# One hand-ordered instruction stream in another order: a cross-attention and MLP block on one core

## The chip, the cores and the metric

The kernel runs on 1 core of one Trainium2 chip. The metric is the device time of one execution in microseconds (us), lower is better. The core has a matrix engine (TensorE, PE in the profile), a vector engine (VectorE, DVE), a scalar engine (ScalarE, ACT), a general engine (GpSimd, POOL) and a queue engine for transfers (SyncE, SP). Each engine runs its own instructions in the order in which the program wrote them, and waits on semaphores for what the others have to deliver.

## The reference

One transformer block in fp32 for 4 batches of 512 rows of width 512, with 16 heads of 32 and a hidden width of 2048:

```python
x = layer_norm(hidden_states, ln1_w, ln1_b)
q, k, v = x @ q_w + q_b, enc @ k_w + k_b, enc @ v_w + v_b      # split into 16 heads of 32
scores = where(mask, q @ k.T / sqrt(32), finfo.min)
out = softmax(scores) @ v                                      # heads side by side again
hidden = (out @ cproj_w + cproj_b) + hidden_states
y = gelu(layer_norm(hidden, ln2_w, ln2_b) @ fc_w + fc_b, approximate=True)
return hidden + y @ proj_w + proj_b
```

## The kernel before

The work is cut into 16 windows w: window w is head group w % 4 (4 heads, 128 columns) of batch w // 4. After four windows a batch goes through the output projection, the second layernorm, the first MLP product (8 chunks c of 256 hidden columns) and, at the end of the kernel, the second MLP product. Batches overlap: while the windows of one batch are in attention, the MLP of the batch before fills TensorE.

The order of everything is a string. `ORDER` (line 60 on) is a list of tokens; the loop at the end of `xattn_block` starts, for each new token, the generator that the table `takes` gives for its name, and each time that the token stands in the string, the generator runs to its next `yield`. So one token is one step, and the place of its n-th occurrence is where its n-th step is written. The schedule is manual: each engine's instructions come in the order of the string, and the waits follow from what a step reads and overwrites. Buffers come from first-in first-out rings (`Ring`): 8 PSUM banks `accs` (a `take` at the first step, a `done` at the last reader), 6 row buffers `rows_of`, 3 staging buffers `stage`. With another order a step can therefore get another bank, and wait for another step to free it.

The tokens that the change and the prediction speak of (step n of a token is written x:4:1.3, counted from 0):

- `k:w`, `q:w`, `v:w` (`prep_k`, `prep_q`, `prep_v`): the projections of a window, 8 matmuls (v: 32) on TensorE, then one ScalarE instruction that frees the bank. `wk:w`, `wq:w`, `wv:w` are the loads of their weights, issued by SP (L331).
- `u:w:t` (`scores`, L516): 8 matmuls for 128 rows t of window w, into four banks. `x:w:t` (`exps`): four steps, each a VectorE instruction (L524) that reads a bank, adds the mask and frees the bank, and a ScalarE exponential (L529).
- `r:w:t` (`turn`): VectorE stream transposes of the exponentials (L537, L544), for odd t also of the reciprocal sums (L541, L547). `d:w:h` (`stay`): POOL copies of a half h of the result (L554). `e:w:h` (`exchange`): 12 SP transfers for the half, swap to swap, that carry the other parts between partitions. `a:w` (`attend`): 32 matmuls (L572) on the exchanged tiles, then one VectorE product (L580). The exchanged tile has one buffer, so the exchange of window w+1 waits for the product of window w.
- `c:b:t` (`cproj`): output projection of 128 rows, with a VectorE add and a POOL transfer to memory. `s1:b`/`s2:b`, `r1:b`/`r2:b`, `n1:b`/`n2:b`, `t1:b:d`/`t2:b:d`: statistics (VectorE, L345), reciprocal roots (POOL, L353 to L361), normalisation (VectorE, L366) and transposes (PE L373, then a VectorE L381 or ScalarE evacuation) of the first and second layernorm. For batches 1 to 3 the first layernorm is applied on an already transposed input: `lb:b` loads the statistics broadcast over partitions (SP, tile `xn<-sd`), `na:b` applies them on POOL (L414), `wa:b` scales on ScalarE (L425).
- `lf:b:c` loads fc weights, `fs:b:c` adds up blocks of them (POOL; VectorE for chunks 2 to 7 of the last batch), `y:b` adds up blocks of the activations (VectorE), `f:b:c` (`fc`, L627) is the product in the Strassen-Winograd form with 7 products for 8 (5 steps of 4 or 8 matmuls), `j:b:c` (`joins`, L652 on) puts its results together on ScalarE and VectorE in a staging buffer, `g:b:c` (`gelu`) applies Gelu there and stores it to memory (a POOL transfer, L674, `gd<-st`), which frees the staging buffer when it has landed.
- `ps`, `pt`, `gs`, `xs`: VectorE sums for the second MLP product `P:b:n` (two levels of the same form), `pj` and `J` its joins.

Of the kernel before, what the change touches and what calls it, by code (L numbers as in the profile page):

```python
# [20 lines left out]
P = 128  # L21
# [51 lines left out]
u:1:3 x:1:3 x:1:3 r:1:2 lt:1 x:1:3 x:1:3 r:1:3 r:1:3
u:2:0 x:2:0 k:4 r:1:3 r:1:3 d:1:0 v:2 d:1:0 d:1:1 k:4 v:4 v:4 v:4 x:2:0 x:2:0 x:2:0 d:1:1 e:1:0 e:1:0 e:1:0
u:2:1
u:2:2 x:2:1 x:2:1 r:2:0 e:1:1 x:2:1 r:2:1 e:1:1 e:1:1 fs:0:1 x:2:1 k:5 r:2:0 r:2:1 x:2:2 wq:5 v:1 fs:0:1 x:2:2 x:2:2
  lb:1 lb:1 r:2:1 r:2:1 k:5 r:2:2 wk:6 na:1 v:5 v:5 x:2:2 lt:1 wv:7 a:1 a:1
u:2:3
u:3:0 x:2:3 r:2:2 wv:6 na:1 e:2:0 na:1 e:2:0 x:2:3 x:2:3 x:2:3 r:2:3 r:2:3 r:2:3 k:6 r:2:3 e:2:0 e:2:1 e:2:1 x:3:0
  e:2:1 na:1 wa:1 d:2:0 wa:1 lf:0:3 wa:1 v:7 d:2:0 wa:1 x:3:0 x:3:0  # L80
u:3:1 q:4 x:3:0 q:4 x:3:1 x:3:1 r:3:0 x:3:1 r:3:0 x:3:1 r:3:1 r:3:1 r:3:1 r:3:1 q:5 wq:7 wv:9 q:5 k:6
u:3:2 x:3:2 x:3:2 d:2:1 x:3:2 x:3:2 d:2:1 a:2 a:2 d:3:0
u:3:3 v:7 wk:7
u:4:0 r:3:2 lx:2 x:3:3 q:7 d:3:0 x:3:3 x:3:3 x:3:3 r:3:2 r:3:3 r:3:3 r:3:3 r:3:3 m:1 k:7 x:4:0 q:7 x:4:0 x:4:0 x:4:0
# [840 lines left out]
```

## Time and profile before

| | |
|---|---|
| median of 3 runs | 757.0 us (755.46 to 757.13) |
| profiled execution, its own time | 760.23 us |
| span of the profiled execution | 758.4 us |
| mean granted TensorE clock | 0.997 |
| PE busy | 747.4 us, 99% of the span, 4413 matmuls |
| DVE busy | 604.9 us, 80% |
| ACT busy | 395.5 us, 52% |
| POOL busy | 374.0 us, 49% |
| transfers | 162.12 MB, mean 214 GB/s |

The profile is of one execution. It lists each engine's busy time, the waits with the instruction that ended them (`<-` names the releaser, which is inferred from semaphore events), the instructions in order of time, and the granted TensorE clock as a share of full speed. A matmul counts as busy while it is in the engine's pipeline, so a busy PE is not a PE at its peak: where the operands of consecutive matmuls come late, the group is only longer. Rows of a timeline hold the start in us from the span's start, the duration, engine, source line, operation, tiles (out<-in), the count of instructions that follow each other, and in brackets the idle time of the engine before them.

### The profile page before, as it was taken

Reading aid. Unit: us, or ns where it says so; the run is one execution under the profiler, and the core shown is the slowest. Engines: PE = TensorE matmul, PEld = TensorE weight load, DVE = VectorE, ACT = ScalarE, POOL = GpSimd, SP = SyncE. Lnnn points to the kernel's source line nnn. Section 1 sums busy time; section 2 is a strip of 40 time slices with the busy share of each in tenths; the row PEclk is TensorE's granted clock in tenths of the full one; section 3 lists DMA queues with packets and bytes.
Section 4 is the critical chain, followed back from the end, with each engine's and each line's share of the span. In section 5 each row is a group of like instructions: output and inputs, shape, how many; then the busy total and the mean of one; then the engine's idle time right before and its main releaser. Section 6 shows DMA issues by size and latency. Waiting matters only on the chain.

```text
span 758.4 us, 13011 instructions
## 1 busy us (share of the span) xinstructions
PE 747.4 (99%) x4413; PEld 526.9 (69%) x4413; DVE 604.9 (80%) x1193; ACT 395.5 (52%) x943; POOL 374.0 (49%) x401
## 2 busy tenths in 40 slices
PE   9999999999999999999999999989999999999998
PEld 6564634457665457674655677674889999999997
DVE  3899989998887979877789876745867998787782
ACT  2666675466887756869566868830334311111110
POOL 1176763744794676497637838581411013231241
PEclk9999999999999999999999999999999999999999
DMA  8689889966979788687796979996455467898485
GB/s 295 230 236 263 236 206 245 237 178 186 271 191 249 193 268 213 175 237 226 189 253 216 253 247 247 261 261 221 147 154 165 159 232 144 233 206 240 96 177 117
DMA packets 72129, 162.12 MB, mean 214 GB/s; under 512 B 11960, under 2 KB 24656, under 8 KB 70400
## 3 DMA queue, kind: packets, MB, share of 16 engines
q1 hardware_dynamic: 56864, 131.44, 60.7%
q0 software_dynamic: 15056, 29.84, 15.7%
q8 instruction: 35, 0.57, 0.3%
q14 instruction: 30, 0.25, 0.1%
q10 hardware_dynamic: 144, 0.02, 0.0%
HBM read 73.95 MB, written 25.18 MB: 131 GB/s over the span
## 4 chain that ended last, share of the span: by engine, by line
PE 67%; DVE 3%; issue 3%; DMA 2%; POOL 1%; ACT 1%; DVEq 0%; ACTq 0%; POOLq 0%
PE acc L627 43%; PE acc L516 5%; PE acc L572 5%; PE acc L447 4%; PE acc L491 4%; PE acc L502 3%; PE acc L479 3%; DMA gd<-st 2%; DVE ptt L524 1%; DVE swap L537 0%; POOL wsum L337 0%; DVE ptt L337 0%; DVE st L334 0%; DVE xn L334 0%; PE acc L373 0%
## 5 line engine op out<-in xcount | busy, mean ns | idle before, releaser
L529 ACT ACTIVATE ptt<-ptt,mn 128x512 f32<-128x512 f32 x256 | 182.7, 715 | 85.8 <-DVE mn L524 85.1
L524 DVE CUSTOM_DVE_ANT_0 ptt<-acc,mix 128x512 f32<-128x512 f32 x256 | 164.8, 680 | 24.9 <-PE acc L516 17.5
L554 POOL COPY swap<-swap 32x1088 f32<-32x1088 f32 x128 | 141.5, 1105 | 72.3 <-DVE mix L580 41.4
L537 DVE STREAM_TRANSPOSE swap<-ptt 128x1024 f32<-128x1024 f32 x64 | 79.0, 1235 | 5.8 <-ACT ptt L529 1.6
L544 DVE STREAM_TRANSPOSE swap<-ptt 128x1024 f32<-128x1024 f32 x64 | 77.9, 1220 | 0.6 <-ACT ptt L529 0.6
L652 ACT COPY xn<-acc 128x128 f32<-128x128 f32 x75 | 18.8, 268 | 107.0 <-PE acc L627 101.2
L516 PE MATMUL acc<-pbt 32*128 32x512 f32 x512 | 73.5, 626 | 1.1 <-ACT pbt L494 0.8
L627 PE MATMUL acc<-ys,wsum 128*128 128x256 f32 x256 | 65.8, 390 | 2.6 <-ACT st L652 2.6
L674 POOL DMA_DIRECT2D gd<-st x32 | 24.1, 761 | 85.5 <-ACT st L672 61.4
L502 PEld LDWEIGHTS acc<-ptt,ext 128*128 128x128 f32 x512 | 59.0, 192 | 8.6 <-DVE mn L524 3.5
L652 ACT COPY st<-acc 128x256 f32<-128x256 f32 x96 | 34.4, 367 | 52.1 <-PE acc L627 45.5
L334 DVE TENSOR_TENSOR st<-acc,st 128x512 f32<-128x512 f32 (+1 forms) x64 | 34.6, 547 | 33.8 <-ACT st L652 23.1
L502 PE MATMUL acc<-ptt,ext 128*128 128x128 f32 x512 | 60.3, 276 | 0.0
L572 PE MATMUL acc<-swap,mix 128*32 128x512 f32 x512 | 58.2, 595 | 1.0 <-POOL swap L554 0.6
L627 PEld LDWEIGHTS acc<-ys,wsum 128*128 128x128 f32 x256 | 48.3, 193 | 15.4 <-ACT st L652 6.6
L479 PE MATMUL acc<-ext,ptt 128*128 128x512 f32 x128 | 58.9, 603 | 0.0
L627 PE MATMUL acc<-yT,pbt 128*128 128x256 f32 x240 | 57.4, 384 | 0.6 <-DVE yT L381 0.6
L491 PE MATMUL acc<-ext,ptt 128*128 128x512 f32 x128 | 57.8, 597 | 0.0
L447 PE MATMUL acc<-mix 128*128 128x512 f32 x128 | 57.3, 598 | 0.0
L672 ACT ACTIVATE st<-st,vec 128x512 f32<-128x512 f32 x64 | 43.9, 718 | 22.1 <-DVE st L334 21.6
L627 PEld LDWEIGHTS acc<-yT,pbt 128*128 128x128 f32 x240 | 44.3, 190 | 15.1 <-DVE mn L524 4.7
L811 POOL DMA_DIRECT2D swap<-xn x18 | 21.9, 1431 | 62.7 <-DVE xn L334 17.7
(129 smaller groups left out, 1386.2 us busy)
## 6 DMA issues: line engine op xcount, KB each, us to landing
swap<-swap SPq DMA_DIRECT2D x384, 136.0 KB, 2.4
gd<-st POOLq DMA_DIRECT2D x32, 512.0 KB, 4.6
swap<-gd SPq DMA_DIRECT2D x12, 1024.0 KB, 6.6
pbt<-fc_w_dram SPq DMA_DIRECT2D x40, 256.0 KB, 4.2
xn<-x_dram SPq DMA_DIRECT2D x32, 256.0 KB, 4.7
ext<-fc_w_dram SPq DMA_DIRECT2D x24, 256.0 KB, 3.1
swap<-xn POOLq DMA_DIRECT2D x18, 256.0 KB, 4.8
ptt<-k_w_dram SPq DMA_DIRECT2D x16, 256.0 KB, 5.1
```

The source lines that it names most:

```text
L447: nc.tensor.matmul(acc, oT[:, g, ts(t, P)], wc[:, g, :], start=(g == 0), stop=(g == NG - 1))
L479: nc.tensor.matmul(acc, S["wk", w][:, d, :], eT[:, d, :], start=(d == 0), stop=(d == ND - 1))
L491: nc.tensor.matmul(acc, S["wq", w][:, d, :], xT[:, d, :], start=(d == 0), stop=(d == ND - 1))
L502: nc.tensor.matmul(acc[:, ts(t, P)], eT[:, d, ts(t, P)], S["wv", w][:, d, :], start=(d == 0), stop=(d == ND - 1),)
L516: nc.tensor.matmul(sc, S["qT", w][r, ts(qt, P)], S["kT", w][r, :], start=True, stop=True)
L524: nc.vector.tensor_tensor_reduce(out=s, in0=accs.held["s", w, qt, h], in1=mb, scale=1.0, scalar=FMAX, op0=ALU.add, op1=ALU.min, accum_out=mn,)
L529: nc.scalar.activation(s, s, AF.Exp, bias=mn, scale=-1.0, accum_out=S["sums", w][:, qt, h : h + 1])
L537: nc.vector.transpose(*two_heads[0])
L544: nc.vector.transpose(*two_heads[1])
L554: nc.gpsimd.tensor_copy(pT[ts(i, HD), i], tb[ts(i, HD), i])
L572: nc.tensor.matmul(av[ts(h, HD), :].rearrange("p (i a q) -> p i a q", i=2 * NI, a=2), v[:, t, ts(h, HD)], p[:, t, h], start=(t == 0), stop ...
L627: nc.tensor.matmul(o, x[:, k], y[:, k], start=(k == 0 and not more), stop=(k == n - 1), skip_group_check=more)
```

## The change

Only the string `ORDER` differs. Both strings hold the same 2367 tokens, each as often, so that every engine runs the same instructions on the same kinds of tile; what differs is the order on each engine, and through the rings which of the equal buffers a step gets. On TensorE 343 of its 458 blocks of matmuls stand at the same place of the sequence. The parts that the prediction speaks of (a `u` token at the head of a line is only how the string is broken into lines):

```diff
--- before.py
+++ after.py
@@ -58,171 +58,167 @@
 ORDER = """
...
-u:2:2 x:2:1 x:2:1 r:2:0 e:1:1 x:2:1 r:2:1 e:1:1 e:1:1 fs:0:1 x:2:1 k:5 r:2:0 r:2:1 x:2:2 wq:5 v:1 fs:0:1 x:2:2 x:2:2
-  lb:1 lb:1 r:2:1 r:2:1 k:5 r:2:2 wk:6 na:1 v:5 v:5 x:2:2 lt:1 wv:7 a:1 a:1
...
-u:3:0 x:2:3 r:2:2 wv:6 na:1 e:2:0 na:1 e:2:0 x:2:3 x:2:3 x:2:3 r:2:3 r:2:3 r:2:3 k:6 r:2:3 e:2:0 e:2:1 e:2:1 x:3:0
-  e:2:1 na:1 wa:1 d:2:0 wa:1 lf:0:3 wa:1 v:7 d:2:0 wa:1 x:3:0 x:3:0
-u:3:1 q:4 x:3:0 q:4 x:3:1 x:3:1 r:3:0 x:3:1 r:3:0 x:3:1 r:3:1 r:3:1 r:3:1 r:3:1 q:5 wq:7 wv:9 q:5 k:6
-u:3:2 x:3:2 x:3:2 d:2:1 x:3:2 x:3:2 d:2:1 a:2 a:2 d:3:0
-u:3:3 v:7 wk:7
-u:4:0 r:3:2 lx:2 x:3:3 q:7 d:3:0 x:3:3 x:3:3 x:3:3 r:3:2 r:3:3 r:3:3 r:3:3 r:3:3 m:1 k:7 x:4:0 q:7 x:4:0 x:4:0 x:4:0
-  e:3:0 s1:2 fs:0:0
-u:4:1 x:4:1 x:4:1 d:3:1 k:7 e:3:0 e:3:0 r:4:0 e:3:1 e:3:1 e:3:1 x:4:1 x:4:1 r:4:0
-u:4:2 x:4:2 x:4:2 fs:0:0 v:6 le:2 lf:0:2 lf:0:2 r:4:1 r:4:1 x:4:2 x:4:2 r:4:1 r:4:1 le:2 d:3:1 r:4:2
-u:4:3 a:3 a:3 x:4:3 x:4:3 r:4:2 c:0:0 c:0:0 d:4:0 x:4:3 lh:0 d:4:0 wq:6 x:4:3 fs:0:0 r:4:3 r:4:3 r:4:3 r:4:3 c:0:1
-  c:0:0 lx:2
-u:5:0 x:5:0 v:5 s2:0 x:5:0 x:5:0 x:5:0 c:0:1 c:0:2 s1:2 d:4:1 le:2 c:0:2 wk:8 wq:9 e:4:0 e:4:0 e:4:0 s2:0 s2:0 cb:0
...
-u:5:1 x:5:1 x:5:1 c:0:3 v:6 v:6 c:0:1 k:8 e:4:1 r:5:0 r:5:0 e:4:1 e:4:1 c:0:2 fs:0:0 c:0:3 q:6 s2:0 x:5:1 x:5:1 c:0:3
...
+u:2:2 d:1:1 v:4 e:1:0 r:2:0 r:2:0 x:2:1 e:1:1 e:1:1 e:1:1 lb:1 x:2:1 r:2:1 r:2:1 v:5 v:5 k:5 x:2:2 r:2:1 r:2:1 x:2:2
+  lb:1 wk:6 a:1 x:2:2 x:2:2 wq:5 r:2:2 wv:7 na:1 na:1 na:1 a:1 d:2:0 lt:1
...
+u:3:0 e:2:0 wa:1 e:2:0 k:6 v:7 wa:1 r:2:3 wa:1 r:2:3 e:2:0 r:2:2 r:2:3 e:2:1 e:2:1 e:2:1 x:3:0 x:3:0 na:1 x:3:0 lf:0:3
+u:3:1 x:3:1 lx:2 wa:1 q:4 q:4 x:3:0 x:3:1 s1:2 d:2:0 r:3:0 x:3:1 x:3:1 q:5 wk:8 r:3:0 wq:7 r:3:1 r:3:1 wv:9 d:2:1
+  d:2:1 r:3:1 k:6
+u:3:2 r:3:1 x:3:2 q:5 a:2 x:3:2 x:3:2 x:3:2 a:2 v:7 r:3:2
+u:3:3 x:3:3 q:7 d:3:0 x:3:3 x:3:3 x:3:3 r:3:2 r:3:3 r:3:3 r:3:3 r:3:3
+u:4:0 m:1 x:4:0 q:7 x:4:0 wk:7 x:4:0 x:4:0 k:7 d:3:0
+u:4:1 x:4:1 x:4:1 d:3:1 e:3:0 e:3:0 e:3:0 r:4:0 r:4:0 k:7 e:3:1 e:3:1 d:3:1 e:3:1 lf:0:2 x:4:1
+u:4:2 x:4:2 x:4:2 x:4:1 r:4:1 x:4:2 r:4:1 r:4:1 r:4:2 fs:0:0 v:6 x:4:2 le:2 le:2
+u:4:3 fs:0:0 fs:0:0 r:4:1 a:3 a:3 x:4:3 x:4:3 le:2 x:4:3 x:4:3 c:0:1 d:4:0 d:4:0 r:4:3 wq:9 r:4:3 r:4:3 r:4:3 wv:8
+  c:0:0 c:0:1 r:4:2 d:4:1 c:0:0 s2:0
+u:5:0 x:5:0 x:5:0 x:5:0 le:2 s1:2 c:0:2
+u:5:1 d:4:1 lh:0 x:5:1 x:5:1 c:0:3 e:4:0 e:4:0 s2:0 e:4:0 wq:6 v:6 x:5:0 q:6 fs:0:0 e:4:1 r:5:0 e:4:1 lx:2 lx:2 r:5:1
...
-u:7:1 x:7:1 x:7:1 j:0:2 lb:2 na:2 wk:10 k:10 lf:0:4 lf:0:4 na:2 k:10 v:10 e:6:0 e:6:0 wa:2 e:6:0 f:0:2 lt:2 lt:2 j:0:2
-  s1:3 f:0:4 r:6:3 d:6:0 j:0:4 fs:0:2 lf:0:6 fs:0:4 r:7:0 x:7:1 x:7:1 r:7:0
...
+u:7:1 lf:0:4 v:10 e:6:0 e:6:0 e:6:0 x:7:1 k:10 k:10 fs:0:2 lf:0:6 wa:2 lt:2 lt:2 f:0:2 j:0:2 d:6:0 r:7:0 f:0:4 x:7:1
+  x:7:1 j:0:4 lh:1 d:6:1 x:7:1 j:0:2
...
-u:14:1 d:13:1 x:14:1 x:14:1 x:14:1 r:14:0 q:15 q:15
-u:14:2 x:14:2 g:1:5 lf:2:1 n2:2 f:1:7 t2:2:3 e:13:1 t2:2:2 lf:2:3 f:1:7 x:14:1 t2:2:0 x:14:2 fs:2:0 j:1:7 t2:2:0
-  e:13:1 t2:2:1 f:1:7 r:14:1 x:14:2 g:1:6 j:1:7 lp:1 x:14:2 t2:2:1 j:1:7 f:2:0 r:14:1 f:1:7 t2:2:3 t2:2:2 fs:2:0 f:2:1
...
-  fs:3:1 c:3:0 lp:5 P:0:2 P:0:2 j:2:7 s2:3 c:3:3 s2:3 g:2:7 lr ps:4 fs:3:1 c:3:2 s2:3 g:2:5 fs:3:0 s2:3 ps:4 c:3:2
-  c:3:3 g:2:5 fs:3:1 r2:3 n2:3 j:2:7 pj:0:1 g:2:7 xs:0:4 g:2:5 n2:3 g:2:6 n2:3 n2:3 t2:3:0 t2:3:0 t2:3:1 t2:3:2 t2:3:3
-  t2:3:3 t2:3:1 f:3:1 t2:3:2 f:3:0 y:3 g:2:7 y:3 y:3 fs:3:0 fs:3:0 f:3:1 ps:6 j:3:1 ps:0 f:3:1 hd:0 j:3:0 gs:0:6 j:3:1
...
-  f:3:2 j:3:0 j:3:0 f:3:3 gs:0:7 pt:6 f:3:0 lf:3:2 ps:6 pj:0:2 P:0:6 j:3:0 g:3:0 j:3:3 fs:3:3 fs:3:3 fs:3:3 fs:3:3
-  j:3:0 g:3:0 g:3:0 fs:3:2 fs:3:2 f:3:3 fs:3:2 g:3:1 ps:2 f:3:3 P:0:5 j:3:3 f:3:3 j:3:3 j:3:3 f:3:2 f:3:3 g:3:1 j:3:2
-  f:3:2 pt:4 j:3:2 fs:3:2 ps:4 pt:4 pt:5 pt:4 P:0:4 hd:0 J:0:1 f:3:2 pj:0:4 pt:4 j:3:3 j:3:3 j:3:2 lf:3:5 g:3:3 f:3:5
...
+u:14:1 x:14:1 x:14:1 r:14:0 x:14:1 x:14:1 q:15
+u:14:2 x:14:2 q:15 f:1:7 f:1:7 j:1:7 x:14:2 d:13:1 e:13:1 e:13:1 n2:2 g:1:6 t2:2:3 t2:2:0 e:13:1 r:14:1 lf:2:3 t2:2:2
+  t2:2:1 t2:2:0 g:1:5 fs:2:0 f:1:7 lf:2:4 x:14:2 j:1:7 x:14:2 t2:2:1 f:2:0 j:1:7 f:1:7 lf:2:3 lp:1 t2:2:3 fs:2:0
+  fs:2:0 f:2:1 j:1:7 g:1:7 fs:2:1 j:2:0 lf:2:2 t2:2:2 y:2 fs:2:1 lf:2:6 y:2 y:2 j:1:7 g:1:7 f:2:1 j:2:1 r:14:1 r:14:1
...
+  j:2:6 la:0:4 xs:0:4 cb:3 P:0:1 a:15 a:15 ps:0 j:2:6 g:2:6 c:3:1 c:3:0 c:3:1 lp:3 ps:2 fs:2:7 la:0:2 la:0:7 c:3:2
+  ps:2 j:2:7 lf:3:1 j:2:7 cb:3 cb:3 gs:0:5 gs:0:6 pt:6 c:3:3 f:2:7 c:3:0 j:2:5 j:2:5 s2:3 j:2:7 s2:3 lp:6 lf:3:0
+  lf:3:0 g:2:5 xs:0:4 fs:3:0 g:2:6 lp:5 P:0:2 lf:3:1 fs:3:1 fs:3:1 c:3:1 c:3:0 lr P:0:2 pj:0:1 g:2:7 g:2:5 ps:4 fs:3:1
+  c:3:2 s2:3 c:3:3 ps:4 s2:3 c:3:2 c:3:3 j:2:7 r2:3 n2:3 g:2:7 fs:3:1 n2:3 n2:3 n2:3 xs:0:4 g:2:7 fs:3:0 t2:3:0 t2:3:1
+  t2:3:1 g:2:5 t2:3:2 t2:3:3 t2:3:0 f:3:1 t2:3:3 t2:3:2 y:3 y:3 y:3 j:3:1 fs:3:0 f:3:0 f:3:1 f:3:1 ps:6 ps:6 fs:3:0
...
+  lf:3:3 j:3:1 j:3:0 j:3:0 g:3:1 f:3:3 f:3:0 j:3:1 fs:3:3 j:3:0 j:3:0 f:3:2 P:0:6 g:3:0 fs:3:3 fs:3:3 fs:3:3 g:3:0
+  ps:0 lf:3:2 fs:3:2 fs:3:2 fs:3:2 j:3:3 f:3:3 f:3:3 P:0:5 g:3:0 j:3:3 f:3:3 j:3:3 j:3:3 f:3:2 j:3:2 f:3:2 hd:0 f:3:3
+  ps:2 ps:6 P:0:4 fs:3:2 j:3:2 g:3:1 f:3:2 J:0:1 ps:4 pt:4 pt:4 j:3:3 pt:4 pt:4 pt:5 lf:3:5 lf:3:5 g:3:3 f:3:5 j:3:2
...
```

The new order moves, among others: `lb:1` directly behind the exchange `e:1:1`; `na:1`'s last step behind the first copies `d:2:0`; `wa:1` between the exponentials of window 3; `s1:2` from window 4 into `u:3:1`; `q:7` in front of `u:4:0`'s matmuls; `wq:6` behind `e:4:0`, and `q:6` in front of `k:8`; `r:7:0` in front of three exps of `x:7:1`; `x:14:1`'s last step in front of `n2:2`'s; the second `gs:0` sum in front of `s2:3`, `fs:3:1` behind `r2:3`; `f:3:2`'s third step in front of `f:3:3`'s last.

260 lines of the change are left out of this document (127 added, 133 removed).

## The prediction

> **What bounds the kernel now.** I read the page's busy times first, then the waits of TensorE, then the stretches in which its stream is not dense, and there the other engines.
>
> ```profile
> PE 747.4 (99%) x4413; PEld 526.9 (69%) x4413; DVE 604.9 (80%) x1193; ACT 395.5 (52%) x943; POOL 374.0 (49%) x401
> ```
>
> TensorE (PE) is busy for 747.4 of the span's 758.4 us. The change leaves its 4413 matmuls as they are, so no order can save more than the time in which the matmul stream is stretched or stands still. The largest standstill is in the list of waits:
>
> ```profile
> PE acc L627 <- ACT st L652: 2.6, 2, 2.3
> ```
>
> One wait of 2.3 us, and it cost more than itself:
>
> ```profile
> 500.57 4.48 PE L627 MATMUL acc<-ys,wsum 128*128 128x256 f32 x12 [2.27 <-ACT st L652]
> ```
> ```profile
> 100.00:128.00 28.00, 27.02 (x148) 11.97 (x150) 27.33 (x62) 19.09 (x51) 13.34 (x13) 1.00 0.84 212
> 497.20:500.60 3.40, 1.14 (x6) 0.68 (x5) 3.37 (x4) 0.45 (x2) 3.11 (x3) 1.00 0.83 260
> 501.60:505.00 3.40, 3.40 (x10) 2.65 (x9) 0.39 (x1) 0.74 (x2) 3.28 (x3) 0.51 0.97 219
> ```
>
> The first row is the fc product that waited (batch 2, chunk 6); the others are stretches of the span with the busy time of PE, PEld, DVE, ACT and POOL, then the granted clock. After the wait TensorE ran 3.40 us at 0.51 of its clock, which lost about half of them, some 1.6; with the 2.3 of standstill (and a little at its edges) the accident cost about 4.1. The profiled execution took 760.2 (span 758.4 and 1.8 around it), 3.2 above the median of 757.0, so I take it that the timed runs have not all had this accident. My sum is made on the profiled execution and applied to the median: the 4.1 are no part of the gain, because the changed order leaves the same ACT copy behind the same staging store there.
>
> The stretch from 100 to 128 shows the other kind of loss. TensorE counts as busy for 27.02 of 28 us, but VectorE (DVE) has 27.33 of 28, and matmuls of the scores are spread out while they wait for their banks:
>
> ```profile
> 101.45 1.14 PE L516 MATMUL acc<-pbt 32*128 32x512 f32 x8
> 103.22 3.64 PE L572 MATMUL acc<-swap,mix 128*32 128x512 f32 x32 [0.64 <-POOL swap L554]
> 106.80 3.62 PE L516 MATMUL acc<-pbt 32*128 32x512 f32 x16
> 110.35 3.70 PE L491 MATMUL acc<-ext,ptt 128*128 128x512 f32 x8
> 113.89 3.60 PE L479 MATMUL acc<-ext,ptt 128*128 128x512 f32 x8
> 117.41 2.37 PE L516 MATMUL acc<-pbt 32*128 32x512 f32 x14
> 120.12 1.12 PE L516 MATMUL acc<-pbt 32*128 32x512 f32 x2 [0.34 <-DVE mn L524]
> 121.17 3.84 PE L502 MATMUL acc<-ptt,ext 128*128 128x128 f32 x32
> 124.94 1.58 PE L516 MATMUL acc<-pbt 32*128 32x512 f32 x8
> 126.45 1.92 PE L572 MATMUL acc<-swap,mix 128*32 128x512 f32 x16
> ```
>
> Starts and lengths of groups of matmuls. Two score blocks (x16) hold TensorE from 106.80 to 110.35, two more (14 and 2) from 117.41 to 121.17, one from 124.94 to 126.45: 8.8 us for five. A block of 8 that waits for nothing takes 1.1 (the first row), so 3.3 are lost, with the 0.64 in front of attend of window 2 some 3.9. This is the largest place that an order can repair. Two smaller ones are at 433-443 and 540-546.
>
> **The change part by part.** Nothing is added or removed; each engine keeps its instructions and durations. So every term below is a step that comes earlier or later, against what waits for it.
>
> *(1) 78 to 128.* Four moves work together. Before, the two broadcast loads of the layernorm statistics (lb:1) stand behind a weight load; now they follow the last exchange of window 1.
>
> ```profile
> 78.67 0.58 SPq L331 DMA_DIRECT2D ptt<-q_w_dram  x1
> 79.36 0.86 SPq L331 DMA_DIRECT2D xn<-sd  x2
> ...
> 108.27 15.12 SPq L331 DMA_DIRECT2D swap<-swap  x24
> ```
> ```profile
> 83.77 1.27 POOL L414 TENSOR_TENSOR ext<-ext,xn 128x512 f32<-128x512 f32 x1 [5.22 <-DMA xn<-sd]
> ```
> ```profile
> 98.67 1.25 DVE L537 STREAM_TRANSPOSE swap<-ptt 128x1024 f32<-128x1024 f32 x1 [1.25 <-POOL swap L554]
> ```
>
> GpSimd (POOL) waited 5.22 us for that load, and from 83.77 to the last copy of window 2 (which attend at 103.22 waits for) it has no gap; the load issued 0.7 earlier (79.36 to 78.67) starts its chain 0.7 earlier. VectorE's 1.25 us wait at 98.67 is for the second of these copies, and POOL's order there (three multiplications, copies, the fourth multiplication, copies) keeps the same work in front of it: 98.0. In the wait VectorE now does layernorm statistics of batch 2 (s1:2.0, 0.84), which stood at 118.5. So VectorE is 0.7 ahead up to 118 and 1.55 from there. Attend of window 2 starts a little earlier, until the landing of its own exchange is the limit; VectorE reaches its result 0.7 earlier, and the exchange of window 3, which waits for that, starts at 107.6 and not at 108.27.
>
> ```profile
> swap<-swap SPq DMA_DIRECT2D x384, 136.0 KB, 2.4
> ```
>
> Its 24 issues take 15.1 us, the last lands 2.4 after its issue: 125.2 before, 124.5 after. On TensorE projection q:7 (3.5 us) moves in front of the first score block of window 4, so that the banks have come free when it is reached; the blocks of 117 to 126 follow VectorE, 0.7 to 1.55 earlier. Attend of window 3 starts at about 124.6, against 126.45: a gain of **1.9**. If the load does not land earlier, only the statistics' 0.84 and part of the bank time are left (0.4); if the landing is no limit, 2.6.
>
> *(2) 180 to 216.* VectorE's first transposes of window 7 now stand in front of three exps (x:7:1.1 to 1.3), not behind one of them.
>
> ```profile
> 206.15 1.25 DVE L537 STREAM_TRANSPOSE swap<-ptt 128x1024 f32<-128x1024 f32 x1 [0.99 <-DMA pbt<-fc_w_dram]
> ```
>
> They wait until 206.15 for an exchange to have read their buffer. One exp (0.6) that filled time before this wait now comes behind it, and the score block and fc product that take its bank are that much later: a loss of 0 (the exchange is early) to 0.6; with the wait of 0.99 that the row shows most of the exp would have fitted in it, so I take the middle, **0.3**.
>
> *(3) 432 to 446.*
>
> ```profile
> 433.59 0.69 DVE L524 CUSTOM_DVE_ANT_0 ptt<-acc,mix 128x512 f32<-128x512 f32 x1 [1.62 <-PE acc L516]
> 434.21 0.08 DVE L524 DVE_READ_ACCUMULATOR2_ANT mn<- 128x1 f32 x1
> 434.21 1.64 DVE L366 TENSOR_SCALAR xn<-xn,mv,rs 128x512 f32<-128x512 f32 x1
> ```
> ```profile
> 440.49 0.70 PE L627 MATMUL acc<-yT,pbt 128*128 128x256 f32 x2 [0.60 <-DVE yT L381]
> ```
>
> VectorE idles for 1.62 until score block u:14:2 has run, then normalises the last row (n2:2.3). An exp of the block before (x:14:1.3) moves into the idle time, and on TensorE one fc step (0.87) moves in front of the transposes that need the row. The row is 0.6 later, its need 0.9 later; behind it VectorE has one exp less, so the transposed blocks come 0.5 to 1.6 earlier. The 0.60 wait goes, with about 0.3 of stretch on either side of it: **1.1** gained (0.2 lost to 1.3 gained, by how long the normalisation takes).
>
> *(4) 522 to 546.*
>
> ```profile
> 536.79 0.55 DVE L366 TENSOR_SCALAR xn<-xn,mv,rs 128x512 f32<-128x512 f32 x1 [1.22 <-POOL rs L361]
> ...
> 538.18 2.31 DVE L366 TENSOR_SCALAR xn<-xn,mv,rs 128x512 f32<-128x512 f32 x3
> ```
> ```profile
> 540.55 1.64 PE L373 MATMUL acc<-ident,xn 128*128 128x128 f32 x13 [0.34 <-DVE xn L366]
> ```
>
> Two g-sums instead of one stand ahead of the statistics (1.1 more), but c:3:3 and a weight-side sum go behind, so the statistics end within a few tenths of the same time. A result join then fills part of the 1.22 wait, and a sum between the first and second normalisation goes behind the fourth: the four rows follow each other and end 0.9 sooner than 540.5, and TensorE's 0.34, with as much again in the next fc step, goes: **0.6** gained (1.4 lost to 1.0 gained).
>
> *(5) The Gelu store at 559 to 566.*
>
> ```profile
> DMA to landing us min/median/max: 3.3/4.6/8.9
> ```
>
> The row is that of the 32 staging stores. The join that needs a store landed is called earlier by TensorE, since f:3:2.2 now precedes the 8 matmuls of f:3:3.4; the store is issued earlier by about as much, since its chunk's last fc step and join move up too. The stall has the same condition as before: **0** (0.5 either way).
>
> *(6) Weight wq:6.* Its load stood ahead of the exchange of window 4; now it stands behind the first half of that exchange, and q:6 is called 3.4 us earlier, in front of k:8.
>
> ```profile
> 131.78 9.16 SPq L331 DMA_DIRECT2D swap<-swap  x12
> 140.98 0.58 SPq L331 DMA_DIRECT2D ext<-encT_dram  x1
> ```
> ```profile
> 149.83 3.60 PE L491 MATMUL acc<-ext,ptt 128*128 128x512 f32 x8
> ```
> ```profile
> DMA to landing us min/median/max: 2.8/4.7/8.8
> ```
>
> The last row is that of the 48 k, q and v weight loads. Half an exchange takes 9.2 us of SyncE's (SP's) queue. With the 1.6 to 1.9 of part (1), the load is issued at about 139.3; q:6 is due at 149.83 less the 3.5 of k:8 (as k:7, 113.89 to 117.41) less 1.9, 144.4. So it is hidden up to 5.1 us of landing, above the median of 4.7: cover, but 0.4 of it. I charge **0.5** for this and the other steps whose margin has shrunk under a microsecond (v:2, v:5, c:0:1, called 3.4 earlier); bounds 0 and the rival's price.
>
> Sum: 1.9 - 0.3 + 1.1 + 0.6 + 0 - 0.5 = 2.8 us. 757.0 - 2.8 = 754.2, or 757.4 on the profiled execution's own time with the accident at 498, 753.3 without.
>
> **What speaks against (3) and (4).**
>
> ```profile
> 434.06 0.73 POOL L674 DMA_DIRECT2D gd<-st  x1
> 434.74 0.82 POOL L337 TENSOR_TENSOR pbt<-pbt 128x256 f32<-128x256 f32 x1
> ```
> ```profile
> L366 DVE TENSOR_SCALAR xn<-xn,mv,rs x20: 504/541/1644, 14.0 to 539.1; 128x512 f32<-128x512 f32 x20
> ```
>
> The normalisation at 434.21 took 1.64 us where the median is 0.54, 1.1 more, while POOL ran beside it. In (4) POOL's weight sum fs:3:1.3 now stands directly behind the reciprocal roots that release the normalisations, and in (3) a weight sum runs when the normalisation comes. Two such collisions in (4) turn its gain of 0.6 into a loss of 0.8 (the gain has 0.8 of slack in it), and one in (3) takes 0.4 of its 1.1: the sum is 1.0 and the time 756.0. This is the first rival.
>
> The Trainium skill, page "SBUF — State Buffer", section "Who interferes with whom", says that VectorE and GpSimd share a pair of ports as an exclusive lock, that whichever issues first blocks the other for the whole instruction, and that tensor_scalar is among the operations that can take it. The 1.64 agrees with that; by the rule alone the time would be this rival's 756.0, not 754.2.
>
> **The rivals.**
>
> *Collisions* (at 536 and 434): 756.0. For it speaks the 1644; against it that of the four rows at 536.79 and 538.18 only one took long (0.55, and 2.31 for three).
>
> *Nothing reaches TensorE.* The exchange is bound by its issue (15.1 us for 24), and VectorE is saturated in 100-128; if the load at 79.36 lands when it did, attend at 103.22 stays, and what is left is filling of idle time on engines that are not the bound: 757.0.
>
> *Slower: q:6 waits for its weight.* Price: a landing of 8.8 (the maximum) leaves TensorE idle for 8.8 - 5.1 = 3.7; the 2.27 at 500.57 already brought the clock to 0.51 for 3.4 us, 1.6 more: 5.3 in all, on 753.7 (the forecast without the charge of (6)), 759.0. The kernel is slower than before as soon as the weight lands some 6.8 us after its issue (1.7 idle, and the clock). For it: the load now goes out in the thick of an exchange. Against it: the median of 4.7.
>
> The Trainium skill, page "TensorE: Matmul & The Clock Gate", section "Why this matters for your kernels", has the clock fall only after gaps of more than about 3 us. The trace disagrees, with 2.27; by the page a landing of 8.0 would cost 2.9 and give 756.6, by the row 4.5 and 758.2.
>
> *More gain.* The bank waits of 106 to 126 and the stretch at 433-446 vanish altogether, and nothing tight costs: 3.9 + 1.3 + 1.0 = 6.2 at most; two thirds of it is 752.9.
>
> **How the numbers follow.** The forecast 754.2 (own range 753.0 to 755.8) gets 0.38, more gain 0.14, collisions 0.12, no effect 0.16, the late weight 0.10, and a new wait of its size at one of the many moved steps that I did not walk through one by one another 0.10. A measurement of this kernel tells from no change about 0.3%, 2.3 us, so faster means under 754.7: 0.14 and two thirds of 0.38, 0.40. Slower, over 759.3: the late weight or the other wait where some of the gains fail too, two thirds of 0.20, 0.13. The rest, 0.47, is the same. The range reaches from most of more gain (751.2, 5.8 of its 6.2) to a late weight with half of part (1) failing (759.9).
>
> **What would show it.** Right: the statistics' load issued straight behind the exchange, attend of window 3 about 1.9 us earlier, no wait of TensorE for yT near 440, normalisations at 536 with the join ahead of them. Wrong: q:6 waiting for SP's queue with the clock at half behind it; normalisations over 1 us; bank waits that reappear in 128-160, where TensorE had none; or a standstill for a staging store in another place.

## The result, and the profile after

The changed kernel took 753.0 us (median of 6 runs, 751.52 to 754.48) against 757.63 for the kernel before in the same session (755.46 to 758.45): ratio 0.9942, 95% interval 0.9923 to 0.9961, so 4.4 us less by the ratio (the medians differ by 4.6). The profiled execution took 752.6, span 750.8. TensorE is still the bound. The engines' busy times, and rows of what is left of TensorE's waits:

```profile
PE 741.9 (99%) x4413; PEld 524.9 (70%) x4413; DVE 603.0 (80%) x1193; ACT 390.1 (52%) x941; POOL 375.1 (50%) x401
```
```profile
PE acc L568 <- DVE rsum L537: 1.5, 1, 1.5
PE acc L851 <- POOL nhalf L840: 1.3, 1, 1.3
PE acc L512 <- ACT pbt L490: 0.8, 1, 0.8
...
PE acc L487 <- DMA ptt<-q_w_dram: 0.3, 1, 0.3
```

The wait at the head of the old list, 2.3 us for an ACT copy into a staging buffer, is gone, and with it the half clock (stretches of the changed kernel, columns as before, and the fc products that had waited):

```profile
100.00:128.00 28.00, 26.21 (x160) 11.30 (x162) 27.68 (x60) 19.28 (x51) 12.42 (x13) 1.00 0.85 220
493.20:496.60 3.40, 3.40 (x18) 2.99 (x17) 3.40 (x5) 1.13 (x4) 1.94 (x3) 1.00 0.92 318
496.60:500.00 3.40, 3.40 (x17) 3.01 (x16) 2.32 (x3) 0.74 (x2) 3.32 (x3) 1.00 0.87 202
```
```profile
494.64 3.62 PE L623 MATMUL acc<-ys,wsum 128*128 128x256 f32 x16
```

(All line numbers of the changed kernel are 4 lower, because its string has 4 lines less; those of the experiments below are lower still for the same reason.)

I laid the starts of equal TensorE blocks of the two traces side by side. The lead of the changed kernel over each stretch, against the forecast:

| stretch | forecast | in this pair of profiles |
|---|---|---|
| (1) 78-128 | +1.9 | +1.2 |
| (2) 180-216 | -0.3 | +1.1 |
| (3) 432-446 | +1.1 | +1.35 |
| the stall at 498 | "no part of the gain" | +4.3 |
| (4) 522-546 | +0.6 | +0.1 |
| (5) 559-566 | 0 | +0.5 |
| the rest (new waits at 264, 310 and 408; small gains) | -0.5 | -0.95 |

They add up to 7.6, the difference of the spans, not to the 4.4 of the ratio: the execution of before that was profiled lay 2.6 above that session's median, that of the changed kernel 0.4 below its own. So the experiments had to tell what belongs to the order from what belongs to one execution.

### The profile page after: what moved, and what is told of

Its sections match the earlier page's. It is cut to its first block, busy times and chain, and to the rows that moved or that the text cites. A ratio compares the mean times of both kernels' runs of the same rounds, so it can differ in the third digit from the quotient of the medians.

```text
span 750.8 us, 13011 instructions
## 1 busy us (share of the span) xinstructions
PE 741.9 (99%) x4413; PEld 524.9 (70%) x4413; DVE 603.0 (80%) x1193; ACT 390.1 (52%) x941; POOL 375.1 (50%) x401
## 4 chain that ended last, share of the span: by engine, by line
PE 51%; DVE 3%; ACT 1%; POOL 1%; issue 1%; DVEq 0%; POOLq 0%
PE acc L623 40%; PE acc L568 3%; PE acc L443 2%; PE acc L512 2%; PE acc L487 1%; PE acc L498 0%; PE acc L475 0%; PE acc L369 0%; DVE xn L362 0%; DVE st L341 0%; DVE swap L533 0%; POOL swap L550 0%; DVE xn L330 0%; DVE ptt L333 0%; ACT ptt L525 0%
## 5 line engine op out<-in xcount | busy, mean ns | idle before, releaser
L512 PE MATMUL acc<-pbt 32*128 32x512 f32 x512 | 71.7, 628 | 0.8 <-ACT pbt L490 0.8
L623 PE MATMUL acc<-ys,wsum 128*128 128x256 f32 x256 | 63.3, 381 | 0.3 <-POOL swap L550 0.3
L512 PEld LDWEIGHTS acc<-pbt 32*128 32x128 f32 x512 | 24.8, 183 | 34.3 <-issue 13.9
```

Of the source, the lines that this page charges most:

```text
L512: nc.tensor.matmul(sc, S["qT", w][r, ts(qt, P)], S["kT", w][r, :], start=True, stop=True)
L623: nc.tensor.matmul(o, x[:, k], y[:, k], start=(k == 0 and not more), stop=(k == n - 1), skip_group_check=more)
```

## The experiments

**The kernel before once more**, and **the stretch 176-217 alone** (all tokens of the kernel before that stand there, sorted as in the changed string).

> The kernel before once more, for a second trace. Theory: the wait of TensorE for the staging store near 498 us and the half clock behind it (4.3 us in the first trace) are an accident of one landing (8.0 us, where the 32 stores had a median of 4.6); here that store lands under 5.7 us and the loss is not there, so the span is about 754 to 756. The losses of order recur: about 4.8 us in the score blocks of 101 to 126, about 1 us at the score block near 207 (u:7:2), about 0.9 us near 440. Rival: the store is late because of what the order puts beside it; then the wait of over 2 us near 498 recurs.

> The kernel before with only the tokens of the stretch 176 to 217 us (u:6:1's middle to a:6) in the changed order. In the two traces TensorE gained 1.1 us there, where I had forecast 0.3 lost. Theory: the gain belongs to the stretch's own order: attend of window 6 starts about 1.1 us earlier than in the kernel before, the time is about 1 us lower (ratio 0.9985), and the first half of the exchange of window 6 lands within 3 us of its last issue. Rival: the gain came from what was done before the stretch; then TensorE gains nothing here.

Once more: 756.46. The stall at 498 came again, with 1.54 of standstill and no half clock. At 206 VectorE waited again, 1.63. The second kernel: 760.59, ratio 1.0058 (1.0037 to 1.0078), slower. The wait at 206 was gone, 1.1 us earlier at 209, but in the next stretch ACT was late and TensorE lost 2.7 at 228-231:

```profile
230.15 1.61 PE L483 MATMUL acc<-pbt 32*128 32x512 f32 x6 [0.96 <-ACT st L624]
```

So this stretch, set into the other order, does not carry its gain along. That the next stretch counts on another state of ACT is the likely reason; no run isolates it.

**The first Gelu store moved.** The store that shares its time with the exchange of window 6 stands at different places in the two strings; I moved it in each to where the other has it.

```diff
 before:  - j:0:1.5 g:0:0.1 g:0:0.2 g:0:1.1      + lf:0:4.1 na:2.1 g:0:0.2 k:10.1
 after:   - na:2.1 g:0:0.2 r:6:3.3               + a:5.1 g:0:0.2 d:6:0.0
```

> The kernel before with one step moved: the Gelu store of batch 0, chunk 0 (512 KB, issued by GpSimd at 189.6 us) behind the second multiplication na:2, so that it goes out behind the first half of window 6's exchange. Theory: this store delayed the exchange (landings of 4 to 6.7 us and an issue of 9.2 us instead of 2.4 and 7.5), and so the transposes of window 7 that waited until 206.15. Then the exchange's first half lands by 202, VectorE's 0.99 us wait goes, and attend of window 6 starts 0.5 to 1 us earlier; ratio about 0.999. Rival: the three weight loads issued just ahead of the exchange delay it; then the landings stay over 4 us, the wait stays and nothing moves.

> The changed kernel with that one store put back ahead of the first copies of window 6, as before. Theory of the store: the exchange's first half again takes over 8.5 us to issue and its last landing is 4 us or more behind its last issue, VectorE waits 1 us or more at the first transposes of window 7, and attend of window 6 starts 1 to 2 us later than in the changed kernel (against 215.82). Rival of the loads: no change, 215.8 within 0.3.

757.26 (1.0011, 0.9993 to 1.003) and 752.79 (0.9948, 0.993 to 0.9966): the store moves nothing that can be seen. (In the trace of the first, VectorE did not wait at 205, as expected, but that proves nothing: the wait comes and goes by itself.) Up to 206 us four of the traced kernels run the same string (before, once more, and the later "reload late" and "stretch 432-446"). VectorE's first transposes of window 7 in two of them, the second and third:

```profile
205.82 1.25 DVE L504 STREAM_TRANSPOSE swap<-ptt 128x1024 f32<-128x1024 f32 x1 [1.63 <-DMA pbt<-fc_w_dram]
```
```profile
205.17 1.22 DVE L504 STREAM_TRANSPOSE swap<-ptt 128x1024 f32<-128x1024 f32 x1
```

The waits were 0.99, 1.63, 0 and 0, TensorE's loss 1.2, 1.8, 0 and 0. Four kernels with the changed order up to there waited 0.01 to 0.03. So what the changed order seems to make safe depends, before, on how late an exchange lands. Averaged over the four it is worth about 0.75, not 1.1. In three more kernels below with the old order in this stretch (the load alone, the stretch 78-128, two moves) VectorE waited for nothing there, which over seven traces makes 0.4. The size is known no better than that; the 0.3 that I forecast as lost was not seen.

**The reload and the store.** At 492 the kernel before issues a 1 MB reload (`la:0:1`, SP, `swap<-gd`) just ahead of the staging store of chunk 4 (`g:2:4`, POOL, `gd<-st`), whose landing frees the buffer for which TensorE's products wait at 498. Issues on SP and POOL, and transfers with their time to landing, before:

```profile
490.51 0.51 SPq L331 DMA_DIRECT2D pbt<-p_w_dram  x1
491.74 0.33 SPq L331 DMA_DIRECT2D swap<-gd  x1
```
```profile
492.05 0.73 POOL L674 DMA_DIRECT2D gd<-st  x1 [3.60 <-ACT st L652]
```
```profile
swap<-gd SPq DMA_DIRECT2D x1, 1024.0 KB, 7.2
gd<-st POOLq DMA_DIRECT2D x1, 512.0 KB, 8.0
```

and in the changed kernel:

```profile
486.02 0.52 SPq L327 DMA_DIRECT2D pbt<-p_w_dram  x1
486.58 2.41 SPq L327 DMA_DIRECT2D swap<-swap  x4
491.52 0.33 SPq L327 DMA_DIRECT2D swap<-gd  x1
```
```profile
489.68 0.73 POOL L670 DMA_DIRECT2D gd<-st  x1 [2.40 <-ACT st L648]
```
```profile
swap<-gd SPq DMA_DIRECT2D x1, 1024.0 KB, 6.1
gd<-st POOLq DMA_DIRECT2D x1, 512.0 KB, 3.7
```

The small load `lp:3` (`pbt<-p_w_dram`) now stands ahead of the last four transfers of an exchange. The reload waits until that exchange has landed, and so goes out 1.84 us behind the store, not 0.31 ahead; the store lands in 3.7 instead of 8.0. Two kernels to test that: the reload put late, and `lp:3` put back.

```diff
 before:  - fs:2:7.0 la:0:1.0 r:15:3.0           + e:15:1.0 la:0:1.0
 after:   - lp:3.0 f:2:6.0 ... e:15:0.2 la:0:1.0 + f:2:6.0 ... e:15:0.2 lp:3.0 la:0:1.0
```

> The order of before with one token moved: the 1 MB reload la:0:1 (SP), which stood right ahead of the staging store g:2:4 at 492, goes out behind the first half of the exchange of the second half-window 15 (at about 499). Nothing is left out. Theory (the store is slow because the reload's packets are in the DMA engines when it starts): the store lands in 3.7 to 5 us instead of 7.3 to 8.4, the TensorE wait for its staging buffer near 498-501 (1.8 to 2.8 us) falls under 0.5, the clock stays at 1.00, the time falls by 2 to 4 us (ratio 0.995 to 0.997). Rival (the store is slow by the exchange or by its own lateness after the Gelu): the store still takes over 7 us, the wait stays, the time is the same within 0.1%.

> The changed order with one token moved back: the small weight load lp:3 goes behind the last part of the exchange e:15:0, as before the change. Nothing is left out. Theory (this small move is what delays the 1 MB reload past the store): the last part of e:15:0 is issued 0.6 us earlier, lands earlier, the 1 MB reload starts within 0.5 us of the store of chunk 4 (or ahead of it), the store takes 6 us or more instead of 3.7, TensorE loses 1 to 4 us near 495 again, the ratio to before is 0.997 to 1.000 instead of 0.994. Rival (the store is fast because it is issued earlier by the order of the Gelus and joins): the store stays at 3.7 to 4.5 us and the ratio at 0.993 to 0.995.

Reload late, in the kernel before:

```profile
swap<-gd SPq DMA_DIRECT2D x1, 1024.0 KB, 6.4
gd<-st POOLq DMA_DIRECT2D x1, 512.0 KB, 3.3
```
```profile
505.13 5.46 PE L594 MATMUL acc<-pbt,swap 128*128 128x256 f32 x16 [5.65 <-DMA swap<-gd]
```
```profile
505.20:508.60 3.40, 3.40 (x8) 2.76 (x9) 0.00 (x0) 0.00 (x0) 3.32 (x3) 0.50 1.02 250
```

The store lands in 3.3, the stall at 498 is gone, as the theory has it. But the second MLP product reads the reloaded data and now waits 5.65 for it, with the clock at half behind: 761.39, ratio 1.0059 (1.0037 to 1.0082). My expectation of the time was wrong because I had not looked at who reads the reload.

`lp:3` back, in the changed kernel:

```profile
489.06 0.52 SPq L298 DMA_DIRECT2D pbt<-p_w_dram  x1
490.27 0.33 SPq L298 DMA_DIRECT2D swap<-gd  x1
```
```profile
490.18 0.73 POOL L641 DMA_DIRECT2D gd<-st  x1 [2.40 <-ACT st L619]
```
```profile
gd<-st POOLq DMA_DIRECT2D x1, 512.0 KB, 7.6
```
```profile
498.30 2.86 PE L594 MATMUL acc<-ys,wsum 128*128 128x256 f32 x12 [2.13 <-ACT st L619]
```

The exchange's issues end at 488.95 here and at 488.99 in the changed kernel; the reload follows 1.3 us later here and 2.5 there. One token back, and the stall is back: 755.63, ratio 0.9978 (0.9958 to 0.9999). So of the 4.4 us some 2.7 hang on the place of one small load (0.6 to 4.8, an estimate from the two intervals).

The timed runs say the same in another way, since each has its mean granted clock on record. One stretch of 3.41 us at half clock, as in the profile before, lowers the mean by 0.002 (1.7 of 758, an estimate). A mean of 0.998 or less stands in 25 of 76 runs of the kernel before, with a median of 758.83 against 756.29 for the other 51. It stands in 5 of 12 runs with `lp:3` back, in none of 6 of the changed kernel, and in one of 26 of the four other kernels in which nothing stalls there (the first Gelu store put back, two moves, the sums moved, three more moves). In the 14 traces the store took 7.3 to 8.5 us in the 8 where the reload is issued between 0.32 ahead of it and 0.09 behind, and 3.3 to 4.0 in the 6 where it is issued 1.2 or more behind.

**The statistics' load alone** (term 1), and **the stretch 78-128 alone**.

```diff
 before:  - wq:5.0 v:1.2 fs:0:1.3 x:2:2.1 x:2:2.2 lb:1.0 lb:1.1     + e:1:1.2 lb:1.0 lb:1.1
```

> The order of before with the two broadcast loads of the statistics of batch 1 (lb:1) moved ahead of the weight load wq:5, right behind the exchange of window 1. Nothing is left out. Theory (the load is the lever of the stretch 78-128): the load lands 1.0 to 1.7 us earlier (without the weight's 256 KB ahead of it it takes 3.3 instead of 4.3), the multiplication on POOL starts at 82.0 to 82.8 instead of 83.77, the exchange of window 3 starts 0.7 to 1.4 earlier, attend of window 3 is 0.7 to 1.2 earlier at 128, with the same losses elsewhere the time falls by 0.7 to 1.2 (ratio 0.9985). Rival (the order of the score blocks, the projection and the statistics in the same stretch is what counts): the exchange of window 3 starts earlier by under 0.4, or attend of window 3 gains under 0.4.

> The order of before with the tokens of the stretch 78 to 128 us in the changed kernel's order, all else as before. Nothing is left out. Theory (what the changed kernel shows at 127, 1.2 us, comes from this stretch's own order): attend of window 3 starts 1.0 to 1.5 us earlier than before, and TensorE keeps at least 0.8 of it to the end, ratio 0.998 to 0.999. Rival (the later stretches need the earlier one's matching order): the gain at 128 is there, but is lost again in new waits before 180, ratio 0.999 to 1.001. Second rival: the gain at 128 is under 0.6 us, and the changed kernel's lead at 127 is from tokens ahead of 78.

The load alone: 755.99, ratio 0.9979 (0.996 to 0.9999), only just clear of no change. Attend of window 3 came 1.1 earlier (here and in the next kernels the difference with which a trace begins, by its first loads, is taken off). The whole stretch gave about as much there, 1.0, and 756.24, 0.9989 (0.9969 to 1.0008), not told from no change. So the load carries term (1), as far as this shows, and the rest of the reordering in that stretch adds nothing that can be seen. In the next kernel the same load gave 0.55 at attend, and in the stretch 432-446, where nothing is moved up to there, attend came 0.4 later than before: the size of this term is known no better than that.

**Two moves together**, in the kernel before: `lb:1` as above, and `lp:3` ahead of `e:15:0.2`. All other 2364 tokens stay.

> The order of before with two small moves on SP's queue alone: the broadcast loads lb:1 ahead of the weight load wq:5 (as in b_lb_early), and the small weight load lp:3 ahead of the last part of the exchange e:15:0. Nothing is left out. Theory (two moves of DMA issues carry most of the changed kernel's gain): the 1 MB reload la:0:1 goes out after the staging store g:2:4, not 0.35 us ahead of it, the store lands in under 5.5 us, the wait near 498 falls from 1.8-2.3 us to under 0.7, the time falls by 1.6 (lb:1) plus 2 to 3 (lp:3), ratio 0.9930 to 0.9955. Rival (the 0.6 us are too few: the reload still starts within half a microsecond of the store): the store takes over 6 us and the ratio stays at 0.997 to 0.999, as with lb:1 alone.

```profile
491.18 0.33 SPq L298 DMA_DIRECT2D swap<-gd  x1
```
```profile
489.98 0.73 POOL L641 DMA_DIRECT2D gd<-st  x1 [3.61 <-ACT st L619]
```
```profile
gd<-st POOLq DMA_DIRECT2D x1, 512.0 KB, 4.0
```
```profile
495.12 3.72 PE L594 MATMUL acc<-ys,wsum 128*128 128x256 f32 x16
```

752.93, ratio 0.9949 (0.9931 to 0.9966): from three tokens a time that is not told apart from the changed kernel's, 0.9942 by the whole reordering.

**The stretch 432-446 alone** (term 3).

> The order of before with the tokens of the stretch 432 to 446 us in the changed kernel's order, all else as before. Nothing is left out. Theory (term 3 of the forecast: the exp fills VectorE's wait and one fc product stands ahead of the transposes): the 0.6 us wait of TensorE for yT near 440 goes, TensorE is 1.0 to 1.4 us earlier at 446 than at 430 against before, ratio 0.9975 to 0.999. Rival (the collision of the normalisation with POOL): the normalisation at 434 takes over 1.2 us and the gain is 0.3 to 0.7. Second rival (given back in the next stretch): the 1.0 to 1.4 are there at 446 and under 0.5 of them at 480.

```profile
432.87 0.55 DVE L333 TENSOR_SCALAR xn<-xn,mv,rs 128x512 f32<-128x512 f32 x1
```
```profile
435.90 1.03 PE L594 MATMUL acc<-ys,wsum 128*128 128x256 f32 x4
...
437.63 1.03 PE L594 MATMUL acc<-yT,wsum 128*128 128x256 f32 x4
497.67 2.86 PE L594 MATMUL acc<-ys,wsum 128*128 128x256 f32 x12 [2.51 <-ACT st L619]
```
```profile
496.90:500.30 3.40, 2.63 (x12) 2.34 (x13) 1.93 (x2) 1.39 (x4) 3.21 (x4) 1.00 0.96 224
500.30:503.70 3.40, 3.40 (x18) 2.99 (x17) 0.69 (x1) 0.37 (x1) 3.21 (x4) 1.00 0.97 209
```

The wait for yT is gone, the normalisation takes 0.55, TensorE gains 1.1 there. The runs, 755.72 and 0.9988 (0.9974 to 1.0003), agree with that but do not show it. The stall at 498 stands as before (2.51; here the clock stayed at 1.00).

**The sums away from the normalisations** (term 4), in the changed kernel, POOL's queue alone; and **a version with three more moves** for the new waits.

```diff
 first:   - r2:3.0 g:2:7.1 fs:3:1.3 ... g:2:7.2 fs:3:0.1 ... fs:3:0.2 ... g:2:6.2
          + fs:3:1.2 fs:3:1.3 fs:3:0.1 c:3:2.2 c:3:3.2 r2:3.0 g:2:7.2 g:2:5.2 g:2:6.2 fs:3:0.2
 second, besides:
          ACT  - k:11.1 j:0:5.0                  + j:0:5.0 k:11.1
          ACT  - g:0:6.0 g:0:7.1 g:0:6.1 t2:1:3.1   + t2:1:3.1 g:0:6.0 g:0:7.1 g:0:6.1
          DVE  - r:13:1.2 r:13:1.3 c:2:2.1 c:2:3.1  + c:2:2.1 c:2:3.1 r:13:1.2 r:13:1.3
```

> The changed order with POOL's queue alone edited at 523-535: the weight sums fs:3:1.3 and fs:3:0.1 go into POOL's idle time ahead of the last two stores of the residual, and fs:3:0.2 behind the three staging stores, so that no weight sum starts while VectorE normalises the four rows of batch 3. Nothing is left out. Theory (the collision rival of the forecast, at this place): the four normalisations take 0.54 us each, 2.2 together instead of 3.96; the transposes at 533 and the fc behind start 0.3 to 0.9 earlier, and the time falls by that much, under what the runs can tell (ratio to before 0.992 to 0.9945). Rival (the long ones come from the DMA issues on POOL or from the reads of the data): two of them still take over 0.9 us, nothing moves.

> The changed order with the edit of POOL's queue at 523-535, and three more moves for the places where the changed kernel's TensorE has new waits: on ACT the join j:0:5.0 goes ahead of the copy k:11.1 (264), the transpose copy t2:1:3.1 ahead of three Gelus (310), and on VectorE the residual sums c:2:2.1 and c:2:3.1 ahead of two masks r:13:1 (408). Nothing is left out. Theory (these waits come from the place in the queue of ACT and VectorE): TensorE's losses of 0.51, 0.74 and 0.57 us fall under 0.2 each, the sum with the normalisations is 1.5 to 2.3, ratio 0.990 to 0.993. Rival (each wait is passed on to the next bank): under 0.7 of it reaches the end, ratio 0.993 to 0.995, as the changed kernel.

The changed kernel's POOL sums (the last row is the third of those that start during the four normalisations at 529.50), and VectorE's rows:

```profile
433.66 0.72 POOL L330 TENSOR_TENSOR wsum<-pbt 128x256 f32<-128x256 f32 x1
...
529.46 0.71 POOL L333 TENSOR_TENSOR wsum<-ext,wsum 128x256 f32<-128x256 f32 x1
...
532.37 0.81 POOL L333 TENSOR_TENSOR wsum<-wsum,ext 128x256 f32<-128x256 f32 x1
```
```profile
203.37 1.25 DVE L533 STREAM_TRANSPOSE swap<-ptt 128x1024 f32<-128x1024 f32 x1
434.13 0.54 DVE L362 TENSOR_SCALAR xn<-xn,mv,rs 128x512 f32<-128x512 f32 x1
529.50 3.96 DVE L362 TENSOR_SCALAR xn<-xn,mv,rs 128x512 f32<-128x512 f32 x4 [1.15 <-POOL rs L357]
```

and with the sums moved (VectorE, POOL, then TensorE):

```profile
529.86 2.58 DVE L333 TENSOR_SCALAR xn<-xn,mv,rs 128x512 f32<-128x512 f32 x4 [1.14 <-POOL rs L328]
```
```profile
529.79 2.39 POOL L641 DMA_DIRECT2D gd<-st  x3
```
```profile
533.08 1.91 PE L340 MATMUL acc<-ident,xn 128*128 128x128 f32 x16
```

3.96 became 2.58 for the four, and the transposes follow without a wait. The three store issues of POOL still ran beside the rows (529.79), so it was the sums, and not these issues, that had cost the time. TensorE gains 0.4 at the transposes and 0.6 to the end of the span. 751.47, ratio 0.9925 (0.9909 to 0.9942), the best of all. The intervals overlap with the changed kernel's, so that it beats that one is not shown.

With three more moves: 751.71, 0.993 (0.991 to 0.9949), span 749.8. The losses at 264 and 408 are gone; that at 310 stayed (0.69 against 0.74), so the copy t2:1:3.1 was not what it waits for, and its cause stays open. About 1 us is saved at these places in the trace, but a wait at 109 costs more than in the changed kernel:

```profile
109.00 1.53 PE L458 MATMUL acc<-ext,ptt 128*128 128x512 f32 x3 [1.20 <-DMA ptt<-q_w_dram]
```

## Why the prediction was right, and where it was not

The time, 753.0 against a forecast of 754.2, was right, but a good part of it for another reason. The changed kernel with `lp:3` back is the forecast's own case, all priced moves with the stall left in: it saves 1.7 (0.9978), not 2.8, though its interval, 0.1 to 3.2, does not exclude that. The stall, which I had left out, is worth the other 2.7. That the time came out so close is luck: a gain that I had ruled out made up for terms that were too large.

*The accident at 498.* The step that failed is "no part of the gain, because the changed order leaves the same ACT copy behind the same staging store". The copy and the store are the same; the landing is not. I looked at who waits for whom and took the store's landing as given, though the row of the stores showed 3.3 to 8.9 us. I also took the accident for a matter of one execution. The standstill came in 8 of the 8 traces where the reload goes out with the store, 1.5 to 2.8 us long; only the half clock comes and goes, in about a third of the timed runs of before.

*(1).* 1.9 forecast, 1.2 found, between 0.4 and 1.7 in five traces with this order. The lever was named rightly, the load. On POOL it gave more than I said, 2.3 us against 0.7 (and 1.8 with the load alone moved), probably since the weight's 256 KB no longer go ahead of it:

```profile
81.47 1.29 POOL L410 TENSOR_TENSOR ext<-ext,xn 128x512 f32<-128x512 f32 x1 [5.28 <-DMA xn<-sd]
```
```profile
106.85 16.40 SPq L327 DMA_DIRECT2D swap<-swap  x24
138.38 0.58 SPq L327 DMA_DIRECT2D ptt<-q_w_dram  x1
```
```profile
107.38 3.67 PE L487 MATMUL acc<-ext,ptt 128*128 128x512 f32 x8 [0.32 <-DMA ptt<-q_w_dram]
...
125.27 3.64 PE L568 MATMUL acc<-swap,mix 128*32 128x512 f32 x32 [1.46 <-DVE rsum L537]
145.22 3.60 PE L487 MATMUL acc<-ext,ptt 128*128 128x512 f32 x8
```

The exchange started 1.4 earlier (106.85), but its 24 issues took 16.40 instead of 15.12, so they ended at 123.25 against 123.39, and attend of window 3, which needs the landing some 2 us behind that, started at 125.27. The mis-sized term is the landing: I moved it by 0.7 with the start of the issues, and their end moved by 0.14. Why the issues took longer is open. TensorE, which is ahead now, waited 1.46 there. The row names a VectorE reciprocal, but in all five traces with this order attend starts 0.24 behind the last landing, so it is the landing that decides.

*(2).* Wrong in sign. I took the wait at 206.15 for part of the order, and it is not there in five of the seven traces with the old order in this stretch. The three exps behind the transposes cost nothing seen, since the transposes do not wait (203.37 above has no bracket).

*(3).* Right: the row at 434.13 took 0.54, no collision, 1.35 gained.

*(4).* Mis-sized, by the first rival, and at the place it named: the sums beside the rows cost 3.96 - 2.58 = 1.4 us of VectorE's time, and 0.1 was left of the 0.6. The Trainium skill, page "SBUF — State Buffer", section "Who interferes with whom", has VectorE and GpSimd exclude each other on a shared pair of ports; the 3.96 and 2.58 agree with it here. At 434, in the same trace, a normalisation took 0.54 while the sum of 433.66 ran (0.25 us of both by the rows, where spans on POOL are rough), so the rule alone does not tell when they meet.

*(5)* came out at +0.5 in this pair, at the edge of its bound.

*(6).* The slower rival did not come, and its price was too high at the low end: it charged the half clock from 1.7 us of standstill on, where 1.54 to 2.51 left the clock at 1.00 in five traces (last section). wq:6 arrived in time: issued at 138.38, it had landed 3.4 us later, and q:6 at 145.22 waits for nothing. Its mechanism came with the sister weight, which I had not priced: q:7 is called 3 us earlier with its load where it was, and waited 0 to 1.20 in five traces, 0.32 here.

Of the new waits at unwalked steps that the forecast gave 0.10, there were three, 0.51 (264), 0.74 (310) and 0.57 (408): small, but together as large as term (1) was forecast.

## What to carry to other kernels

Price the landing of a transfer, not only its issue: when one kind of transfer shows 3.3 to 8.9 us, look at what is in flight beside each slow one. Here one small load, moved past four transfers of a queue, let a store run ahead of a large reload and was worth more, by the medians, than the rest of a reordering of 2367 tokens (2.7 against 1.7). And profile the kernel before more than once: what differs between two traces of the same order is no gain of the new order, and what recurs in all of them is no accident.

## What the runs showed of the hardware

The 512 KB store at 492 lands in 3.3 to 4.0 us when the 1 MB reload from another queue is issued 1.2 us or more behind it, and in 7.3 to 8.5 when it is issued from 0.32 ahead of it to 0.09 behind, nothing in between in 14 traces. The Trainium skill, page "DMA: Bandwidth & Descriptors", section "Queues, rings and completion order", says that each DMA engine takes turns between the queues that have work for it, packet by packet. Turns with one other queue would about double the 3.3 to 4.0, to 6.6 to 8.0 (an estimate from the rows), which agrees with half of the eight; the other four took 8.2 to 8.5. The reload loses less by it: it lands in 6.2 to 7.7 us in the 8 traces and in 5.1 to 6.4 in the 6.

The clock is no function of the gap's length alone: 2.51 of standstill left it at 1.00 (the stretch 432-446 alone), 2.27 brought it to 0.51 (before), 5.65 to 0.50. The Trainium skill, page "TensorE: Matmul & The Clock Gate", section "What's actually happening", has a window of about 3.4 us that runs freely, so that the place in it matters. The traces agree: in each, the granted clock changes only at whole multiples of 3.41 us after the first entry of its clock record, 145 of them up to 501.64 in the trace before, where it falls to 0.50 until 505.05. Cut into these windows, what counts is TensorE's idle time inside one:

| kernel | window | idle in it, us | clock in the next |
|---|---|---|---|
| stretch 78-128 | 495.30-498.71 | 2.8 | 0.50 |
| reload late | 498.48-501.89 | 2.4 | 0.50 |
| before | 498.23-501.64 | 2.3 | 0.50 |
| the first Gelu store moved | 498.22-501.63 | 2.0 | 0.50 |
| stretch 176-217 | 499.78-503.19 | 1.65 | 1.00 |
| once more | 496.41-499.82 | 1.5 | 1.00 |
| the load alone | 496.40-499.81 | 1.4 | 1.00 |
| stretch 432-446 | 496.38-499.79 | 1.3 | 1.00 |
| `lp:3` back | 494.00-497.41 | 1.2 | 1.00 |

The 2.51 of the stretch 432-446 falls half into one window and half into the next, the 2.27 of before into one. So the clock halved after windows with 2.0 us or more of idle time and not after those with 1.65 or less; where between them the limit lies, no trace shows. A window need not be idle throughout for it.
